# A two-layer attention block on one core: sums of the second softmax in float32r, and a new order at both ends of the run

## The chip, the cores and the metric

The kernel runs on one core of a Trainium2 chip. The metric is the device time in microseconds (us) of one launch of the whole program; lower is better. Ten runs of the kernel before are given, and one further execution that the hardware profiler took.

## The reference, cut to what matters

Eight images of 32 x 32 positions (N = 1024) and 512 channels pass through two layers; everything is float32.

```python
x = x + L0(_gn(x))      # 16 heads of 32: qkv = x @ w_qkv, softmax(q k^T * 32**-0.5) v, @ w_proj + b_proj
x = x + L1(_gn(x))      # 4 heads of 128: Wq, Wk, Wv, softmax((q k^T + position logits) / sqrt(128)) v, @ Wo
```

`_gn` is a group normalisation over groups of 16 channels. The position logits of layer 1 come from two learned tables, one for rows and one for columns of the image. A softmax is computed without subtracting a maximum: exponentials, their sums over the keys, and a division at the end.

## The kernel before, in words

**Layout.** The kernel works with channels on the partitions and tokens along the free axis, in tiles of 128 x 512. Eight blocks of 128 x 4 x 1024 floats (the pool `block`) hold activations; what is not needed for a while is written to DRAM (`put_away`, L213) and read back (`fetch`, L221). PSUM has eight banks: four as one tile `ps` for the first attention's scores, one `acc` for its output and its sums, and three named `bank` for everything else (L81).

**Projections.** Each 512 x 512 weight matrix is applied by a Strassen-like scheme with seven products instead of eight (`seven`, L341). Its inputs are the quarter blocks of the activation and four sums of these, made by four VectorE instructions of 128 x 1024 in `forms` (L324), and the matching four sums of the weights, made by `Matrix.add_up` (L137). A matrix takes 14 *products* (two units of seven); each is 8 matmuls of 32 columns, one per column group of the array (`by_columns`, L308).

**First attention** (`attention_0`, L519): 64 steps per batch (four groups of four heads, two halves of the queries, eight key tiles). A step issues 8 score matmuls into `ps` (L532), one exponential of 128 x 2048 on ScalarE (L540), 4 output matmuls into `acc` (L551) and one addition of 128 x 2048 to the running sums `es` on VectorE (L562). After eight steps `finish` (L568) multiplies `es` with a matrix of ones (L572), which both sums over the partitions and spreads the result, and `normalise` (L489) divides.

**Second attention** (`attention_1`, L637): also 64 steps per batch (four heads, two halves, eight key tiles). A step issues one score matmul of 128 x 512 in float32 (L647), one in float32r that adds the position logits (L648), an exponential of 128 x 512 (L650), one output matmul (L659) for the step before, and an addition to `es` (L670). After eight steps `finish` (L676) issues one float32 matmul of `ones` and `es` into a third of the `bank` tiles (L679), a copy to SBUF, two transposes with a reciprocal between, and a multiplication on GpSimd (L517).

**The order of the work** is written out by hand with Python generators. The main loop (L936) runs nine rounds. In round b, `side_by_side` (L862) steps through the first attention of batch b, and between its steps advances a chain of other work until `done` has caught up with `total`: the output projection of layer 0 for batch b-1 (`after_0`), that of layer 1 for batch b-2 (`after_1`), the second layer's projections for batch b-1 (`second`), its second attention, and the first layer's projections for batch b+1 (`before_0`). Each piece of that chain yields a cost: 2 for a product, and 0 for a step of the second attention. So the second attention of rounds 1 to 6 stands as one unbroken run of 64 steps between two steps of the first attention. In round 7, the last one with a first attention, `total` is 28 + 28 + 76 - 4 = 128, all first-attention steps stand beside the projections, and the second attention of batch 6 follows them. Round 8 has no first attention at all.

Inside the second attention of rounds 1 to 6, `woven(..., 4, 6)` (L850, L963) advances `load` (L696) of the next batch after every sixth step: transposes of the input, its statistics, the group normalisation, and then `forms` as a whole.

**The start** (`load_first`, L719) is different: the first batch is transposed on TensorE in two halves; the first half's four banks are copied by ScalarE (L745), the second half's by ScalarE and VectorE in turn (L747). Then come the statistics (L248), `put_away` to DRAM, the group normalisation in place, and `forms`. After that the program text fetches WQ and WK of layer 0 and lets VectorE make their sums (L146, called from L920). The framework's scheduler orders the instructions of each engine by when it thinks that they are ready, unless a helper (`issue_after`, `keep_in_program_order`) binds one to another.[...]

Of the kernel before, what the change touches and what calls it, by code (L numbers as in the profile page):

```python
# [17 lines left out]
P = 128  # L18
# [9 lines left out]
def quick_path(  # L28
# [52 lines left out]
    def bank(name, shape=None):  # L81
        return psum.tile(shape or [P, NB], F32, tag="bank", name=name, bufs=3)
# [1 line left out]

    ident = consts.tile([P, P], F32, tag="ident", name="ident")
    make_identity(nc, ident)
    ones = consts.tile([P, P], F32, tag="ones", name="ones")
    nc.gpsimd.memset(ones, 1.0)
    bproj_sb = consts.tile([P, CC], F32, tag="bproj_sb", name="bproj_sb")
    with nc.allow_non_contiguous_dma(reason="512 values, once"):  # L90
        nc.gpsimd.dma_start(bproj_sb, b_proj.rearrange("(cc p) -> p cc", p=P))
# [212 lines left out]
    in_place = [False]  # L304

    half_done = [None]

    def by_columns(out, weights, moving, start, stop, open_sum=False):  # L308

# [11 lines left out]
                tc.keep_in_program_order(ins)  # L321
        in_place[0] = False

    def forms(x, name):  # L324


        a11, a12 = x[:, :HC, :NB], x[:, HC:, :NB]
        a21, a22 = x[:, :HC, NB:], x[:, HC:, NB:]
        s1, s2, s4 = [
            mem.tile([P, HC, NB], F32, tag=f"form{i}", name=f"f{i}_{name}", bufs=1) for i in (1, 2, 4)  # L330
        ]
        nc.vector.tensor_add(s1, a21, a22)
        nc.vector.tensor_sub(s2, s1, a11)
        nc.vector.tensor_sub(a21, a11, a21)
        nc.vector.tensor_sub(s4, a12, s2)
        return [a11, a12, s4, a22, s1, s2, a21]

    def snapshot(tag, name):
        return mem.tile([P, NB], F32, tag=tag, name=name, bufs=3 if tag == "e1" else 2)
# [294 lines left out]
                if i % 2:  # L634
                    yield 0

    def attention_1(q, k, v, posT, b):  # L637

        steps = [(h, c, j) for h in range(H1) for c in range(NH) for j in range(NT)]
        state = {}  # L640

        def front(h, c, j):
            name = f"1_{b}_{h}_{c}_{j}"
            ps = bank(f"ps_{name}")
            keys = slice(j * P, (j + 1) * P)
            queries = slice(c * NB, (c + 1) * NB)
            nc.tensor.matmul(ps, k[h][:, keys], q[:, h, queries], start=True, stop=False)  # L647
            nc.tensor.matmul(ps, sel_flat[:, keys], posT[:, h, queries], start=False, stop=True)  # L648
            e = mem.tile([P, NB], F32, tag="e1", name=f"e_{name}", bufs=3)
            nc.scalar.activation(e, ps, AF.Exp, scale=1.0 / math.sqrt(D1))  # L650
            return e

        def back(h, c, j, e):
            name = f"1_{b}_{h}_{c}_{j}"
            if j == 0:
                state["acc"] = bank(f"acc_{name}")
                state["first"] = e
            acc = state["acc"]
            nc.tensor.matmul(  # L659
                acc,  # L660
                v[:, j, h * D1 : (h + 1) * D1],
                e,
                start=(j == 0),
                stop=(j == NT - 1),
            )
            if j == 1:
                state["esum"] = mem.tile([P, NB], F32, tag="es1", name=f"es_{name}", bufs=2)
                nc.vector.tensor_add(state["esum"], state["first"], e)  # L668
            elif j > 1:
                nc.vector.tensor_add(state["esum"], state["esum"], e)  # L670
            if j < NT - 1:
                return
            nc.scalar.copy(q[:, h, c * NB : (c + 1) * NB], acc)
            state["ended"] = (h, c, state["esum"])

        def finish(h, c, esum):  # L676
            name = f"1_{b}_{h}_{c}"
            su = bank(f"sums_{name}")
            nc.tensor.matmul(su, ones, esum, start=True, stop=True)  # L679
            normalise(q[:, h, c * NB : (c + 1) * NB], su, name)  # L680

        pending = None
        for at in steps:
            e = front(*at)
            ended = state.pop("ended", None)
            if pending is not None:
                back(*pending)
            pending = (*at, e)
            if ended is not None:
                finish(*ended)  # L690
            yield 0
        back(*pending)
        yield 0
        finish(*state.pop("ended"))

    def load(b, st):  # L696

        x = xT = None
        parts = [(cc, h) for cc in range(CC) for h in range(NH)]
        ahead = [load_blocks(b, *parts[i]) for i in range(2)]  # L700
        for i, (cc, h) in enumerate(parts):
            xs = ahead.pop(0)
            if i + 2 < len(parts):
# [12 lines left out]
        st["xn"] = forms(x, f"xn0_{b}")  # L716
        yield 0

    def load_first(st):  # L719

        rows = block("x_rows", [P, NT, C])
        for t in range(NT):
            queue = nc.scalar if t % 2 else nc.sync
            queue.dma_start(rows[:, t, :], xf[0, t * P : (t + 1) * P, :])
        WV0.fetch(nc.sync)
        x = block("x0T_0")
        xT = chunks(x)
        for h in range(NH):
            if h == 0:
                whole = psum.tile([P, CC, NB], F32, tag="ps", name="turned_0", bufs=1)  # L730
                banks = [whole[:, cc, :] for cc in range(CC)]
            else:
                banks = [bank(f"turned_1_{cc}") for cc in range(CC - 1)]
                banks.append(psum.tile([P, NB], F32, tag="acc", name="turned_1", bufs=1))
            for t in range(NT // NH):
                for cc in range(CC):
                    nc.tensor.transpose(
                        banks[cc][:, t * P : (t + 1) * P],
                        rows[:, h * (NT // NH) + t, cc * P : (cc + 1) * P],
                        ident,  # L740
                    )
            for cc in range(CC):
                part = xT[cc][:, h * NB : (h + 1) * NB]
                if h == 0 or cc % 2:
                    nc.scalar.copy(part, banks[cc])  # L745
                else:
                    nc.vector.tensor_copy(part, banks[cc])  # L747

        idle = psum.tile([P, CC, NB], F32, tag="ps", name="idle", bufs=1)
        for t in range(6):  # L750
            nc.tensor.matmul(idle[:, t % CC, :], ident, rows[:, t, :], start=True, stop=True)
        for cc in (1, 0, 3, 2):
            statistics(st, xT, cc, "0_0")
        st["kept"] = put_away(xT, "0_0")
        run(group_norm(st, xT, "0_0"))
        st["xn"] = forms(x, "xn0_0")
# [129 lines left out]
    def later(part, *args):  # L886

        yield from part(*args)
# [28 lines left out]
    WV0.add_up(nc.gpsimd, nc.gpsimd, keep=True)  # L917
    for m in (WQ0, WK0):
        m.fetch(nc.sync)
        m.add_up(nc.vector, nc.gpsimd, keep=True)  # L920
    fill_sel()
    stream = Stream(plan)

# [6 lines left out]
    def at_once(do):  # L930
        do()
        return
        yield

    run(before_first(states[0]))
    for b in range(B + 1):  # L936
# [11 lines left out]
        if last is not None:  # L948
            norm = norm_1(b - 1, last, (lambda: half_done[0]) if past is not None else None)
            rest.append(after_0(b - 1, last, forms_past if past is not None else None))  # L950
            total += PRODUCT
            if past is not None:
                rest.append(woven(later(after_1, b - 2, past), norm, 3, 3))
                total += PRODUCT
            else:
                rest.append(chain([ALONE], (cost + ALONE for cost in norm), marked()))
                total += 4 * ALONE
            rest.append(later(second, b - 1, last))
            total += SECOND
            if here is not None and coming is None:  # L960
                rest.append(at_once(forms_0))
                total -= 4
            rest.append(woven(later(lambda st: attention_1(*st.pop("at")), last), incoming, 4, 6))  # L963
        else:
            rest.append(woven(rest_of_first(here), incoming, 0, 2))
            total += PRODUCT
# [502 lines left out]
```

## Time and profile before

| what | value |
|---|---|
| median of 10 runs | 3904.27 us (3901.32 to 3908.26) |
| profiled execution | 3907.13 us, its span 3905.3 us |
| TensorE (PE) busy | 3811.1 us, 98% |
| VectorE (DVE) busy | 2518.1 us, 64% |
| ScalarE (ACT) busy | 1724.3 us, 44% |
| GpSimd (POOL) busy | 621.3 us, 16% |
| mean granted TensorE clock | 0.993 |

A float32 matmul shows as two matmul records, a float32r one as one. [...]what a matmul costs in a row of others is the distance from its start to the start of the next. A group's line gives the engine, the operation, output and inputs by name, the count, busy time and mean length, and then the idle time before it with what ended that.

### The profile page before, as it was taken

How to read it: one execution, taken by the hardware profiler on the slowest of the kernel's cores; microseconds unless marked ns; L12 is line 12 of the kernel's file. 1: busy time of each engine (PE TensorE's matmuls, PEld its weight loads, DVE VectorE, ACT ScalarE, POOL GpSimd, SP SyncE). 2: the span in 40 equal slices, each digit the busy share in tenths (PEclk: the TensorE clock that was granted, in tenths of full speed). 3: DMA queues.
4: the chain of work that ended last, by engine and by line, in shares of the span. 5: the costliest groups of instructions: out<-in, count | busy, mean ns of one | idle time of the engine just before them, and what ended most of it. 6: DMA issues, size and time to landing. Idle time of an engine off the chain costs nothing.

```text
span 3905.3 us, 79833 instructions
## 1 busy us (share of the span) xinstructions
PE 3811.1 (98%) x34478; PEld 1370.9 (35%) x34478; DVE 2518.1 (64%) x2905; ACT 1724.3 (44%) x1767; POOL 621.3 (16%) x400
## 2 busy tenths in 40 slices
PE   8999899999999999999999999999999999999998
PEld 3222244232442224432343323433234332244353
DVE  5767775577746867458664686656865568754544
ACT  2554453444434454344544445344453445543132
POOL 1341001121111210112101121111210112011101
PEclk9999999999999999999999999999999999999999
DMA  5231120133201422023220241103311123110401
GB/s 169 76 107 42 47 61 6 39 116 70 61 2 51 118 60 55 9 90 84 49 55 16 92 94 38 46 22 98 87 44 34 29 93 69 32 63 18 123 17 23
DMA packets 482984, 234.73 MB, mean 60 GB/s; under 512 B 269600, under 2 KB 461376, under 8 KB 481600
## 3 DMA queue, kind: packets, MB, share of 16 engines
q1 hardware_dynamic: 470992, 213.74, 20.3%
q0 software_dynamic: 2608, 13.70, 1.0%
q8 instruction: 274, 4.49, 0.5%
q10 hardware_dynamic: 9024, 2.10, 0.3%
q14 instruction: 86, 0.70, 0.1%
HBM read 170.72 MB, written 58.72 MB: 59 GB/s over the span
## 4 chain that ended last, share of the span: by engine, by line
PE 84%; DVE 9%; ACT 3%; issue 2%; POOL 1%; DMA 0%; SPq 0%; DVEq 0%; POOLq 0%; ACTq 0%
PE ps L647 11%; PE acc L659 11%; PE ps L532 11%; PE acc L551 10%; PE y_k L312 4%; PE y_v L312 4%; PE y_q L312 4%; PE ps L648 3%; PE x_v L312 3%; PE x_k L312 3%; PE z_k L312 3%; PE x_q L312 3%; PE z_v L312 3%; PE z_q L312 2%; ACT e L540 2%; DVE es L562 2%
## 5 line engine op out<-in xcount | busy, mean ns | idle before, releaser
L540 ACT ACTIVATE e<-ps 128x2048 f32<-128x2048 f32 x512 | 961.6, 1878 | 845.0 <-PE ps L532 608.1
L562 DVE TENSOR_TENSOR es<-es,e 128x2048 f32<-128x2048 f32 x384 | 890.7, 2319 | 400.3 <-ACT e L540 397.5
L532 PE MATMUL ps<-q,k 32*64 32x512 f32 x8192 | 578.1, 616 | 35.5 <-ACT e L540 35.4
L650 ACT ACTIVATE e<-ps 128x512 f32<-128x512 f32 x512 | 305.7, 597 | 586.2 <-PE ps L648 549.4
L551 PE MATMUL acc<-e,v 128*32 128x512 f32 x4096 | 548.0, 607 | 0.4 <-ACT su L495 0.4
L647 PE MATMUL ps<-q,k 128*128 128x512 f32 x1024 | 523.6, 593 | 0.3 <-DVE posT L633 0.3
L659 PE MATMUL acc<-e,v 128*128 128x512 f32 x1024 | 521.9, 592 | 0.0
L517 POOL TENSOR_TENSOR q<-q,su 128x512 f32<-128x512 f32 x128 | 214.3, 1674 | 1567.2 <-DVE su L513 1540.5
L670 DVE TENSOR_TENSOR es<-es,e 128x512 f32<-128x512 f32 x384 | 291.9, 760 | 264.0 <-ACT e L650 262.5
L648 PE MATMUL ps<-posT,sel 128*128 128x512 f32 x512 | 406.6, 794 | 0.0
L647 PEld LDWEIGHTS ps<-q,k 128*128 128x128 f32 x1024 | 193.6, 190 | 246.1 <-issue 240.6
L532 PEld LDWEIGHTS ps<-q,k 32*64 32x64 f32 x8192 | 120.5, 130 | 432.4 <-ACT e L540 215.3
L659 PEld LDWEIGHTS acc<-e,v 128*128 128x128 f32 x1024 | 193.1, 189 | 146.7 <-issue 105.0
L551 PEld LDWEIGHTS acc<-e,v 128*32 128x32 f32 x4096 | 81.5, 108 | 414.1 <-issue 366.3
L560 DVE TENSOR_TENSOR es<-e,e 128x2048 f32<-128x2048 f32 x64 | 174.4, 2725 | 40.3 <-ACT e L540 40.3
L497 DVE STREAM_TRANSPOSE tu<-su 128x512 f32<-128x512 f32 x128 | 90.6, 708 | 137.5 <-ACT su L495 137.3
L495 ACT COPY su<-sums 128x512 f32<-128x512 f32 x128 | 74.9, 585 | 152.5 <-PE sums L572 79.7
L648 PEld LDWEIGHTS ps<-posT,sel 128*128 128x128 f32 x512 | 97.3, 190 | 122.5 <-issue 122.5
L668 DVE TENSOR_TENSOR es<-e,e 128x512 f32<-128x512 f32 x64 | 44.2, 691 | 145.7 <-ACT e L650 145.7
L633 DVE TENSOR_TENSOR posT<-pp,posT 32x512 fp32r<-32x512 f32 x128 | 112.0, 875 | 32.1 <-ACT posT L628 30.8
L421 POOL TENSOR_TENSOR k<-b_k,p_k 128x512 f32<-128x512 f32 x32 | 51.2, 1599 | 476.9 <-ACT p_k L386 474.9
L628 ACT CAST posT<-pp 32x512 fp32r<-32x512 f32 x128 | 106.0, 828 | 45.3 <-PE pp L615 44.2
(195 smaller groups left out, 4517.9 us busy)
## 6 DMA issues: line engine op xcount, KB each, us to landing
w_qkv<-ws_qkv SPq DMA_DIRECT2D x168, 128.0 KB, 2.5
d<-x0T SPq DMA_DIRECT2D x32, 512.0 KB, 3.5
x1T<-d SPq DMA_DIRECT2D x32, 512.0 KB, 5.5
d<-x1T SPq DMA_DIRECT2D x32, 512.0 KB, 3.6
x2T<-d SPq DMA_DIRECT2D x32, 512.0 KB, 6.0
w_qkv<-in_L_conv_w_qkv SPq DMA_DIRECT2D x126, 128.0 KB, 2.2
out<-ot SPq DMA_DIRECT2D x240, 64.0 KB, 2.0
xs<-in_x SPq DMA_DIRECT2D x224, 64.0 KB, 2.6
```

Source lines behind the costliest of these rows:

```text
L312: ins = nc.tensor.matmul(out[columns, :], weights[:, columns], moving, start=start, stop=stop, skip_group_check=open_sum,)
L517: nc.gpsimd.tensor_tensor(dst, dst, su, op=ALU.mult)
L532: nc.tensor.matmul(ps[some, r, :], k[m][rows, j * P + 64 * i : j * P + 64 * i + 64], q[m][rows, h * NB : (h + 1) * NB], start=True, stop=True,
L540: nc.scalar.activation(e, ps, AF.Exp, scale=D0 ** -0.5)
L551: nc.tensor.matmul(acc[r * D0 : (r + 1) * D0, :], v[:, j, c0 : c0 + D0], e[:, r, :], start=(j == 0), stop=(j == NT - 1),)
L560: nc.vector.tensor_add(state["esum"], state["first"], e)
L562: nc.vector.tensor_add(state["esum"], state["esum"], e)
L647: nc.tensor.matmul(ps, k[h][:, keys], q[:, h, queries], start=True, stop=False)
L648: nc.tensor.matmul(ps, sel_flat[:, keys], posT[:, h, queries], start=False, stop=True)
L650: nc.scalar.activation(e, ps, AF.Exp, scale=1.0 / math.sqrt(D1))
L659: nc.tensor.matmul(acc, v[:, j, h * D1 : (h + 1) * D1], e, start=(j == 0), stop=(j == NT - 1),)
L670: nc.vector.tensor_add(state["esum"], state["esum"], e)
```

## The change

It has four parts.

- **Last first-layer attention.** In round 7 the first 32 steps of the second attention now cost 1 each instead of 0, and `total` becomes 28 + 28 + 76 + 32 = 164. So `side_by_side` places about a fifth of the first attention's steps among these 32. `forms_0`, which needs the finished first attention, moves to after step 40 of the second attention.
- **The second layer's sums.** `finish` copies `es` to float32r on ScalarE (`greater`), subtracts that from `es` on VectorE (`rest`), and two steps later issues two float32r matmuls with `ones`, into the four-bank `ps` tile, which the first attention isn't using at that time. The first three finishes of round 7 keep the old form, since there it is in use.
- **The next batch's forms.** `forms` becomes a generator, `forming`, that yields after each of its four instructions, each bound behind the latest addition to `es`. `load` is advanced every fifth step instead of every sixth.
- **The start.** ScalarE copies all eight banks, in the order 0, 2, 1, 3; statistics follow the same order; the sums of WQ and WK are bound behind the last instruction of `forms`.

```diff
+    ones_r = consts.tile([P, P], F32R, tag="ones", name="ones")
+    nc.gpsimd.memset(ones_r.bitcast(F32), 1.0)
+    ones = ones_r.bitcast(F32)
...
-    def forms(x, name):
+    def forming(x, name, behind=None):
...
+        for op, out, one, other in (
+            (nc.vector.tensor_add, s1, a21, a22),
+            (nc.vector.tensor_sub, s2, s1, a11),
+            (nc.vector.tensor_sub, a21, a11, a21),
+            (nc.vector.tensor_sub, s4, a12, s2),
+        ):
+
+            late = behind() if behind is not None else None
+            with tc.issue_after(late.ins) if late is not None else nullcontext():
+                last_form[0] = op(out, one, other)
+            yield 0
         return [a11, a12, s4, a22, s1, s2, a21]
...
-    def attention_1(q, k, v, posT, b):
+    def attention_1(q, k, v, posT, b, beside=0):
...
         def finish(h, c, esum):
             name = f"1_{b}_{h}_{c}"
-            su = bank(f"sums_{name}")
-            nc.tensor.matmul(su, ones, esum, start=True, stop=True)
+            if (h * NH + c + 1) * NT < beside:
+                su = bank(f"sums_{name}")
+                nc.tensor.matmul(su, ones, esum, start=True, stop=True)
+                normalise(q[:, h, c * NB : (c + 1) * NB], su, name)
+                return
+
+            yield
+
+            greater = mem.tile([P, NB], F32R, tag="rec", name=f"sg_{name}", bufs=2)
+            nc.scalar.copy(greater, esum)
+            rest = mem.tile([P, NB], F32R, tag="rec", name=f"sr_{name}", bufs=2)
+            nc.vector.tensor_sub(rest, esum, greater.bitcast(F32))
+
+            yield
+            yield
+
+            su = psum.tile([P, HB, NB], F32, tag="ps", name=f"sums_{name}", bufs=1)[:, 0, :]
+            nc.tensor.matmul(su, ones_r, greater, start=True, stop=False)
+            nc.tensor.matmul(su, ones_r, rest, start=False, stop=True)
             normalise(q[:, h, c * NB : (c + 1) * NB], su, name)

         pending = None
+        ending = []
         for at in steps:
             e = front(*at)
-            ended = state.pop("ended", None)
             if pending is not None:
                 back(*pending)
             pending = (*at, e)
-            if ended is not None:
-                finish(*ended)
+            for part in ending:
+                next(part, None)
+            if "ended" in state:
+                ending = [finish(*state.pop("ended"))]
+                next(ending[0], None)
             yield 0
         back(*pending)
         yield 0
-        finish(*state.pop("ended"))
+        run(finish(*state.pop("ended")))
...
-        st["xn"] = forms(x, f"xn0_{b}")
-        yield 0
+        st["xn"] = yield from forming(x, f"xn0_{b}", lambda: added[0])
...
-            for cc in range(CC):
+            for cc in (0, 2, 1, 3):
                 part = xT[cc][:, h * NB : (h + 1) * NB]
-                if h == 0 or cc % 2:
-                    nc.scalar.copy(part, banks[cc])
-                else:
-                    nc.vector.tensor_copy(part, banks[cc])
+                nc.scalar.copy(part, banks[cc])
...
-        for cc in (1, 0, 3, 2):
+        for cc in (0, 2, 1, 3):
             statistics(st, xT, cc, "0_0")
...
-        m.add_up(nc.vector, nc.gpsimd, keep=True)
+
+        with tc.issue_after(last_form[0].ins):
+            m.add_up(nc.vector, nc.gpsimd, keep=True)
...
-            if here is not None and coming is None:
-                rest.append(at_once(forms_0))
-                total -= 4
-            rest.append(woven(later(lambda st: attention_1(*st.pop("at")), last), incoming, 4, 6))
+            shared = here is not None and coming is None
+            attention = later(
+                lambda st, steps: attention_1(*st.pop("at"), steps), last, H1 * NT if shared else 0
+            )
+            if shared:
+
+                attention = woven(
+                    (int(at < H1 * NT) for at, _ in enumerate(attention)),
+                    at_once(forms_0),
+                    H1 * NT + NT,
+                    H1 * NH * NT,
+                )
+                total += H1 * NT
+            rest.append(woven(attention, incoming, 4, 5))
```

More of the change, by code (lines that the diff above doesn't have):

```diff
@@ L86, in quick_path @@
     make_identity(nc, ident)
-    ones = consts.tile([P, P], F32, tag="ones", name="ones")
-    nc.gpsimd.memset(ones, 1.0)
+    ones_r = consts.tile([P, P], F32R, tag="ones", name="ones")
+    nc.gpsimd.memset(ones_r.bitcast(F32), 1.0)
+    ones = ones_r.bitcast(F32)
     bproj_sb = consts.tile([P, CC], F32, tag="bproj_sb", name="bproj_sb")
@@ L306, in quick_path @@
     half_done = [None]
+    last_form = [None]
+    added = [None]
     def by_columns(out, weights, moving, start, stop, open_sum=False):
@@ L331, in forms, with whole @@
         ]
[L332 to L335, printed above, removed]
-        return [a11, a12, s4, a22, s1, s2, a21]
+        for op, out, one, other in (
[8 more added lines that the diff above has]
+            yield 0
+        return [a11, a12, s4, a22, s1, s2, a21]
+    def forms(x, name):
+        got = []
+        def whole():
+            got.append((yield from forming(x, name)))
+        run(whole())
+        return got[0]
     def snapshot(tag, name):
@@ L669, in back @@
             elif j > 1:
-                nc.vector.tensor_add(state["esum"], state["esum"], e)
+                added[0] = nc.vector.tensor_add(state["esum"], state["esum"], e)
             if j < NT - 1:
```

## The prediction

> **What bounds the kernel now.** I read the page's busy times and its chain of waits, then busy time by stretch, then the order of matmuls inside the second attention, and last VectorE's timeline at the start.
>
> ```profile
> span 3905.3 us, 79833 instructions
> ...
> PE 3811.1 (98%) x34478; PEld 1370.9 (35%) x34478; DVE 2518.1 (64%) x2905; ACT 1724.3 (44%) x1767; POOL 621.3 (16%) x400
> ...
> PE 84%; DVE 9%; ACT 3%; issue 2%; POOL 1%; DMA 0%; SPq 0%; DVEq 0%; POOLq 0%; ACTq 0%
> ```
>
> TensorE is the bound: 98% busy, 84% of the chain. An edit gains only by removing matmul time or by filling the 94 us in which TensorE idles. Where these lie, TensorE alone, in stretches (stretch, length, busy time, granted clock):
>
> ```profile
> 1033.60:1165.40 131.80, 131.80 (x344) 1.00 0.11 27
> 2704.50:2926.10 221.60, 218.90 (x2521) 1.00 0.27 66
> 3176.50:3463.00 286.50, 271.98 (x3076) 0.99 0.21 56
> 3463.00:3594.90 131.90, 131.90 (x343) 1.00 0.05 19
> ```
>
> The first and fourth are runs of the second attention: no idle time at all. The second is round 6 beside projections: 2.7 us idle. The third is round 7: 14.5 us idle, of which the waits for its stretch give 9.6 to the wide exponential (L540) and 2.6 to the last sums. That is all the first part can win.
>
> Inside the second attention (start, length, engine, line, ...):
>
> ```profile
> 1083.24 1.02 PE L647 MATMUL ps<-q,k 128*128 128x512 f32 x2
> 1083.70 0.79 PE L648 MATMUL ps<-posT,sel 128*128 128x512 f32 x1
> 1084.33 1.02 PE L659 MATMUL acc<-e,v 128*128 128x512 f32 x2
> 1085.19 1.02 PE L679 MATMUL sums<-es,ones 128*128 128x512 f32 x2
> 1086.05 1.02 PE L647 MATMUL ps<-q,k 128*128 128x512 f32 x2
> ```
>
> Starts, not lengths, give the cost. Sums: 1086.05 - 1085.19 = 0.86 us. A whole step is 1.945 us (1081.29 to 1083.24), two float32 matmuls take 1.71 of it, so the float32r one takes 0.23.
>
> The start, on VectorE:
>
> ```profile
> 14.67 0.20 DVE L249 BATCH_NORM_AGGREGATE mv<-st 128x2 f32<-128x12 f32 x1
> 16.88 1.68 DVE L146 TENSOR_TENSOR prep_qkv<-prep_qkv 128x512 f32<-128x512 f32 x1 [2.02 <-DMA prep_qkv<-in_L_conv_w_qkv]
> ...
> 24.55 0.16 DVE L285 SCALAR_TENSOR_TENSOR var<-back 128x4 f32<-128x4 f32 x1
> 25.88 2.98 DVE L292 TENSOR_SCALAR x0T<-x0T,back,rstd 128x1024 f32<-128x1024 f32 x4 [1.16 <-POOL rstd L289]
> 28.77 0.69 DVE L146 TENSOR_TENSOR prep_qkv<-prep_qkv 128x512 f32<-128x512 f32 x1
> 29.38 1.22 DVE L332 TENSOR_TENSOR f_xn<-x0T 128x1024 f32<-128x1024 f32 x1
> ```
>
> The statistics stand behind a sum of weights that waits for its DMA; TensorE stands idle for 10.39 us before its first product at 26.79.
>
> [...]0.23 for one float32r pass, 0.43 for each half of a float32 matmul. [...]sums followed by 32-column products take 0.95 us (1164.42 to 1165.37), not 0.86. [...]on SP's queue WQ lands at 16.86 and the four stores of x0T, issued after it, 1.1 to 1.3 us apart from 18.13 to 21.82. [...]
>
> **Part 1, round 7.** The built order has 53 first-attention steps before the second attention's first step and 11 among its next 31. The same 70 products (5 matrices of 14) now share 53 steps instead of 64. No matmul is removed, so the gain is idle time only. Two points are measured: 64 steps with 70 products idle 14.5 us, of which 2.6 is the wait of the last sums at the end of the stretch; round 6 has 42 steps with its 70 products and idles 2.7. In a line between 11.9 and 2.7, 53 steps give 7.3. The end wait goes, since second-attention matmuls now stand there. Among the mixed steps TensorE needs 2.03 + 2.8 x 1.95 = 7.5 us per first-attention step, VectorE 2.3 + 2.8 x 0.76 = 4.4, ScalarE 1.9 + 2.8 x 0.6 = 3.6, so I expect little idleness there, 0.5. But in the built order a single one of the eight score matmuls stands twice in front of full-width sums; alone, it takes its whole 0.86 us: 1.7. New idle time 7.3 + 0.5 + 1.7 = 9.5; gain 14.5 - 9.5 = **5.0**. Bounds: -2 (mixed steps stall as the old ones did) to 12. The moved `forms_0`, 4.9 us of VectorE, lands where VectorE is under half busy (59 of 132) and TensorE waits for nothing; without that cover it would cost up to 4.9. On SP's queue the fetch of x1T (four DMAs, landing in 6 us) moves behind weights that are released as TensorE goes on; the data is wanted tens of us later: nothing.
>
> **Part 2, the sums.** 61 of 64 are changed. Two float32r passes: [...]0.47 by the trace's 0.23; a weight load of 0.19 (L648's) hides under each. I take 0.47; saved 0.86 - 0.47 = 0.39 in the 53 finishes that have more steps behind them: 20.7. The added copy (an ACT copy of that size takes 0.585; a cast, L628, 0.83) and subtraction (0.69; a float32r one, L633, 0.875) wait behind exponentials and additions; queued behind the copy is the next exponential, behind the subtraction the next addition. By the old run's times, around 575 us, `rest` is ready at 578.2 and its matmul would stand at 580.7: 2.5 us of cover, so nothing. Without it each 1 us of lateness costs 53.
>
> At the **end of a run** there is no cover. The built order is: last `acc`, *one* 32-column product matmul, both sums, the other seven. The last addition ends at 1164.12, copy 1164.73, `rest` 1165.5. The lone matmul takes 0.86, its column group running by itself, then comes a wait of about 0.1, sums 0.47, and two more changes of tiling at 0.1. Against 0.86 before, that is 0.86 + 0.1 + 0.47 + 0.2 - 0.86 = 0.77 lost, 7 times: -5.4. In round 8 the end is followed by a chain through ScalarE, VectorE and GpSimd for which TensorE idles anyway; it starts 0.75 later: -0.75. Sum 20.7 - 5.4 - 0.75 = **14.5**. Bounds: 2 (passes of 0.28, casts at the dear rates, 1.5 lost at each end) to 25 ([...]ends that gain too).
>
> **Part 3, the next batch's forms.** 4 instructions of 1.22 us spread over VectorE inside a run without idle time, before and after: **0**. They end about five steps (10 us) before the run does; if that were lost, the first product would wait up to 1.2 us, 6 times. The bound upward is 0 too: there is no wait to remove.
>
> **Part 4, the start.** VectorE loses two copies and gets statistics without the weights' sums: it would finish `var` near 16.5 instead of 24.7. GpSimd's `rstd` stands behind WV's sums and the issue of their store there (until 18.9), so about 20 instead of 25.8. But the normalisation overwrites x0T, and so waits for its stores. WK's fetch of 1 MB now stands ahead of them in SP's queue: at WQ's pace (2.5 us) that moves them from 18.1...21.8 to 20.7...24.5, and the store of WV's sums (landing 26.35 before) takes a share: I take 27 for the last. Then the second of the forms, which TensorE's third product needs, is ready at 27 + 0.75 + 2.4 = 30.2 instead of 32.3. Before, TensorE's 14 products end at 55.58, at 1.73 each as if begun at 31.4; now two are done by 30.2, as if begun at 26.7: 4.7. Against that, the eight sums of WQ and WK (0.65 each) now stand on VectorE ahead of the first evacuation of y, until 38, and the product that accumulates onto y would be due at 36.9: 1.6 lost. **3**; bounds 0 to 7.
>
> **Sum.** 5.0 + 14.5 + 0 + 3 = 22.5. Against the profiled execution (3907.1, 1.8 more than its span) 3884.6; the profiled one is 2.9 over the median of the ten, so from 3904.3: **3882**.
>
> **Rivals.**
> - *Nothing is lost at the edges.* TensorE overlaps the lone matmul with what follows, stores land early, mixed steps have no idle time: 10 + 22 + 7 = 39, 3865. For it: VectorE has slack everywhere. Against: waits in the built order[...].
> - *The edits hardly reach their place.* Round 7 keeps its idle time (VectorE's work is the same, 222 of 286 us), stores hold the start: 0 + 10.5 + 0.5 = 11, 3893. For it: VectorE's load beside 53 steps is nearly what it was beside 64.
> - *`rest` comes late every time, slower.* The sums stand in TensorE's order; if copy and subtraction slip behind the next batch's normalisation and forms, each finish stalls TensorE. From 22.5 / 53 = 0.42 us per finish, that is `rest` 2.9 us later than laid out, the kernel is slower; at 4 us later, 53 x 1.5 = 80 is lost: 3962. Against: VectorE is 57% busy there (75 of 132), and no single instruction exceeds 1.3 us.
>
> **Chances.** Forecast 0.56, first rival 0.20, second 0.20, third 0.04. A measurement of this kernel can tell about 0.2% (7.8 us) from no change. The forecast's own spread is 3875 to 3889; half the first rival's cases and most of the second's are taken in to reach 8 in 10: 3864 to 3895. Faster 0.92: the first three cases, less the slowest of the second; same 0.05; slower 0.03.
>
> **What would show it.** Right: runs of the second attention of about 129.5 us instead of 131.8, sums starting 0.47 before what follows, one gap near 0.1 and a lone x_q matmul at each end; idle time of 9 to 10 us in round 7; the first product near 21 to 23 and WQ's first at about 52.5. Wrong: idle time before the sums inside a run, or float32r passes over 0.3 apart; and the sum would be wrong if round 7 with its 32 steps isn't 5 us shorter than before.

## The result, and the profile after

The changed kernel takes **3875.25 us** (median of 8 runs, 3871.06 to 3880.73), the kernel before 3903.7 us over the 28 runs that stand beside it. The ratio is 0.9931, with a 95% interval from 0.9922 to 0.994: 28 us or 0.7% less. The forecast was 3882 with a range of 3864 to 3895, so the sign and the range held. The gain is 6 us larger than the 22.5 that was worked out, and its parts don't lie where the sum put them.

The profiled execution took 3880.94 us. On its page, the span and the busy times:

```profile
span 3879.1 us, 79880 instructions
...
PE 3797.7 (98%) x34478; PEld 1373.7 (35%) x34478; DVE 2556.8 (66%) x2964; ACT 1761.1 (45%) x1830; POOL 614.2 (16%) x400
```

TensorE remains the bound, with exactly as many matmul records as before: a float32 matmul leaves two, and so do the two float32r ones that replace it. What was removed is time in the records and idle time between them. In stretches (stretch, length, busy time of TensorE, granted clock, DMA share, GB/s):

```profile
1026.88:1155.14 128.26, 128.26 (x339) 1.00 0.11 27
2690.10:2909.60 219.50, 216.79 (x2504) 1.00 0.27 66
3161.40:3405.00 243.60, 240.57 (x2777) 1.00 0.23 58
3405.00:3564.40 159.40, 159.40 (x622) 1.00 0.07 26
```

The first is a run of the second attention from its first scores to the end of its last output matmul, again without idle time; before, such a run took 130.97 (1033.61 to 1164.58). The second is round 6, with 2.7 us of idle time as before. The third and fourth together are round 7: 3.0 us of idle time in the part beside projections, where 14.5 had been and 9.5 were forecast, and none in the part that the two attentions share.

A round is measured here from the start of its first product to that of the next round's. The changed kernel is 3.3 us ahead at WQ's first product and 3.4 at the start of round 1. Round 1 gains 3.3, of which 1.4 isn't the edit's: TensorE runs 10.2 us of that round at half clock, and 17.1 in the trace before. Rounds 2 to 6 gain 1.9 each (16.2 at the end of round 6), round 7 gains 14.2 (30.4), and round 8 gives 4.1 back: 26.3, the difference of the two spans. Of the 14.2, 0.95 is only moved: the last sums of round 7's run stood ahead of round 8's first product before, and stand behind its first matmul now.

Inside the second attention, the new sums (start, length, engine, line, operation):

```profile
1080.72 1.02 PE L679 MATMUL acc<-e,v 128*128 128x512 f32 x2
1081.17 0.80 PE L715 MATMUL sums<-sg,ones 128*128 128x512 f32 x1
1081.81 0.40 PE L716 MATMUL sums<-sr,ones 128*128 128x512 f32 x1
1082.05 1.02 PE L667 MATMUL ps<-q,k 128*128 128x512 f32 x2
```

From the output matmul's start to the next score matmul's are 1082.05 - 1080.72 = 1.33 us; without sums between them it is 0.86 (1084.33 to 1085.19 in the prediction's lines of the kernel before). The pair costs 0.47, as forecast, in place of 0.86. No wait stands before it.

At the end of a run, before and after:

```profile
1162.61 1.97 PE L659 MATMUL acc<-e,v 128*128 128x512 f32 x4
1164.42 1.02 PE L679 MATMUL sums<-es,ones 128*128 128x512 f32 x2
1165.37 1.92 PE L312 MATMUL x_q<-x0T,w_qkv 128*32 128x512 f32 x16
1167.22 0.69 PE L532 MATMUL ps<-q,k 32*64 32x512 f32 x8
```

```profile
1153.16 1.97 PE L679 MATMUL acc<-e,v 128*128 128x512 f32 x4
1155.07 1.05 PE L316 MATMUL x_q<-x0T,w_qkv 128*32 128x512 f32 x2
1156.04 0.51 PE L715 MATMUL sums<-sg,ones 128*128 128x512 f32 x1
1156.39 0.39 PE L716 MATMUL sums<-sr,ones 128*128 128x512 f32 x1
1156.71 1.92 PE L316 MATMUL x_q<-x0T,w_qkv 128*32 128x512 f32 x14
1158.55 0.69 PE L552 MATMUL ps<-q,k 32*64 32x512 f32 x8
```

The lone x_q matmul (two records) holds TensorE for 0.97 us, the sums for 0.67, the other seven for 1.84 together. From the start of the last outputs to the next scores are 5.39 us; before, 1162.61 to 1167.22, 4.61. So 0.78 is lost at each end; 0.77 was forecast. The gap of about 0.1 that the forecast had there doesn't show; the lone matmul is longer by as much than the 0.86 it was given. The 0.67 is what the forecast's 0.47 and its two times 0.1 for a change of tiling come to; the 0.1 was its estimate from one place in the trace before, 0.95 us for sums ahead of 32-column products against 0.86 for those inside a run.

The start, on VectorE:

```profile
19.11 0.16 DVE L286 SCALAR_TENSOR_TENSOR var<-back 128x4 f32<-128x4 f32 x1
20.83 0.81 DVE L293 TENSOR_SCALAR x0T<-x0T,back,rstd 128x1024 f32<-128x1024 f32 x1 [1.56 <-DMA d<-x0T]
...
27.19 0.81 DVE L293 TENSOR_SCALAR x0T<-x0T,back,rstd 128x1024 f32<-128x1024 f32 x1 [2.87 <-DMA d<-x0T]
28.04 1.23 DVE L345 TENSOR_TENSOR f_xn<-x0T 128x1024 f32<-128x1024 f32 x1
29.30 1.23 DVE L345 TENSOR_TENSOR f_xn<-f_xn,x0T 128x1024 f32<-128x1024 f32 x1
```

The normalisation now waits for the stores of what it overwrites (the bracket names the DMA d<-x0T), the last until 27.19, and the second form is ready at 30.5: 27 and 30.2 were forecast.

### The profile page after: what moved, and what is told of

Same layout as the page of the kernel before. It is cut to its first block, busy times and chain, and to the rows that moved or that the text cites. A ratio compares the mean times of both kernels' runs of the same rounds, so it can differ in the third digit from the quotient of the medians.

```text
span 3879.1 us, 79880 instructions
## 1 busy us (share of the span) xinstructions
PE 3797.7 (98%) x34478; PEld 1373.7 (35%) x34478; DVE 2556.8 (66%) x2964; ACT 1761.1 (45%) x1830; POOL 614.2 (16%) x400
## 5 line engine op out<-in xcount | busy, mean ns | idle before, releaser
L441 POOL TENSOR_TENSOR v<-b_v,p_v 128x512 f32<-128x512 f32 x32 | 50.8, 1586 | 443.1 <-ACT p_v L406 440.4
```

## The experiments

They start from the kernel before with one part of the change alone, then with two, then from the changed kernel with one detail altered. Each text on record states its own theories. In a sum of medians each difference carries some 4 us either way, so the traces' own distances are read beside the times.

**Part 1 alone.** Only the round-7 sharing and the place of `forms_0` are taken from the diff (its last hunk).

> The kernel before with part 1 alone (32 second-attention steps of cost 1, the first attention's last steps among them, the old sums). Theory A, from the trace after: the idle time of round 7 falls from 14.5 us to about 3 because 53 instead of 64 steps share the projections, and nothing else of the change is needed for it: 9 to 12 us less than before. Theory B, as the prediction had it: 5 us less, and what the trace after shows beyond that in round 7 comes of the other parts together (the freed third bank in the mixed steps). If B, this run gains 4 to 6.

Measured: 3890.77 us against 3900.63, ratio 0.9972 (0.9962 to 0.9982), 9.9 us less. Theory A. In round 7, from its first to the next round's first product, the trace is 14.1 us shorter. What TensorE waited for beside the projections (engine, tile and line, releaser: us, times, longest), the longest of the kernel before and then all but one of this run:

```profile
PE ps L532 <- ACT e L540: 9.6, 8, 2.7
PE sums L572 <- DVE es L562: 2.6, 1, 2.6
```

```profile
PE ps L532 <- ACT e L540: 1.4, 2, 1.2
PE sums L572 <- DVE es L562: 1.3, 1, 1.3
```

Of 9.6 us for the wide exponential and 2.6 for the last sums, 1.4 and 1.3 are left, with another 0.3 elsewhere. Part 1 by itself takes away the idle time, 11.5 us of it where 5.0 was forecast. The trace gains 2.6 more than that: 1.7 because the trace before has a stretch of half clock in round 7 and this one has none, and 0.9 that isn't traced.

**Part 2 alone.** `ones_r`, the new `finish` and its stepping, and nothing else; without part 1 all 64 finishes are of the new form.

> The kernel before with part 2 alone (the float32r sums, in every round). Theory A, the prediction's working: 56 finishes with steps behind them at 0.39 us, seven run ends at -0.77, the last at -0.75, so 15.7 us less than before; a run of the second attention of 128.3 us up to its last acc. Theory B: the sums also free a tile of the bank pool, and waits outside the runs shrink; then 18 or more. Theory C: the float32r pair costs more once the other parts are away (rest late because the forms stand as a block on VectorE): 10 or less.

Measured: 3897.87 us, ratio 0.9993 (0.9984 to 1.0001): 2.8 us, hardly to be told from nothing. Theory A is out. Theory C has the size right, and not the place: nothing waits for the sums. Runs of the second attention up to the last output take 129.7 us in rounds 1 to 6, against 128.26 in rounds 7 and 8, where no next batch's `load` stands beside them. VectorE, ScalarE and TensorE around the one idle place of the run in round 2:

```profile
1073.36 2.30 DVE L335 TENSOR_TENSOR x0T<-x0T 128x1024 f32<-128x1024 f32 x1
...
1075.58 0.68 DVE L671 TENSOR_TENSOR es<-es,e 128x512 f32<-128x512 f32 x1
...
1076.18 1.21 DVE L336 TENSOR_TENSOR f_xn<-x0T,f_xn 128x1024 f32<-128x1024 f32 x1
...
1077.31 0.68 DVE L671 TENSOR_TENSOR es<-es,e 128x512 f32<-128x512 f32 x1
1078.08 0.62 ACT L688 CAST sg<-es 128x512 fp32r<-128x512 f32 x1 [3.31 <-DVE es L671]
1078.61 0.59 ACT L651 ACTIVATE e<-ps 128x512 f32<-128x512 f32 x1
...
1079.25 1.12 PE L660 MATMUL acc<-e,v 128*128 128x512 f32 x2 [1.22 <-ACT e L651]
```

It is read from below. TensorE waits 1.22 us for an exponential. The exponential stands on ScalarE behind the copy `sg`, and the copy, after 3.31 us of idling, waits for the last addition to `es`. That addition stands on VectorE behind the fourth form, another addition and the third form. The third form is also slow: it takes 2.30 us where a form by itself takes 1.2, and so it is in all six runs (2.29 to 2.30). A multiplication on GpSimd started 0.36 us ahead of it each time (the last section has what this does). So about 1.1 us of the lateness comes of that meeting and the rest of the order; no run takes the two apart. In the kernel before, the forms make the additions late too (one starts at 1078.33, though its exponential ended at 1077.34), but there every exponential of that stretch waits for its scores alone, and TensorE doesn't idle.

**Part 3 alone.** `forming` and the fifth step instead of the sixth.

> The kernel before with part 3 alone (the next batch's forms one by one, load advanced every fifth step). Theory A: the run of the second attention has no idle time before, so nothing: within 1.5 us of before. Theory B: the forms as a block delayed the first steps after the run, and spreading them takes 1 us from each of six rounds: 5 us less.

Measured: 3901.18 us, ratio 0.9997 (0.9989 to 1.0006): nothing, as forecast. Theory A.

**Parts 2 and 3 together.**

> The kernel before with parts 2 and 3 together (float32r sums, and the next batch's forms spread over VectorE), parts 1 and 4 left out. Alone, part 2 gave 2.8 us and part 3 nothing. Theory A: they are worth more together than apart, because the forms as a block on VectorE delay the last addition, ScalarE's copy waits for it, and the next exponential, queued behind the copy, makes the output matmul late by 1.2 us once in each of six runs. Then the runs of the second attention in rounds 1 to 6 shrink from 129.7 to 128.3 us, and the time is 11 to 13 us below the kernel before. Theory B: parts 2 and 3 don't act on each other; runs stay at 129.7 and the time is 2 to 4 us below the kernel before. Theory C: the prediction's 14.5 for part 2 was right, and part 3 adds something besides: 14.5 or more.

Measured: 3891.64 us against 3901.23, ratio 0.9974 (0.9964 to 0.9984): 9.6 us less, where the two alone sum to about 2.3. The runs of all rounds are 128.2 to 128.3 us long and have no idle time. Theory A holds in the trace, and in time but for its last 1.4 us; B is out. Every form inside the runs takes 1.2 us here, so the run takes away the block and the meeting with GpSimd at once; nor does it tell the spreading from the fifth step.

**Part 2 with the copy moved.** If the wait goes by way of the exponential behind the copy, it should go without part 3 too, once the copy stands behind that exponential:

```diff
-            nc.scalar.activation(e, ps, AF.Exp, ...)
+            risen.append(nc.scalar.activation(e, ps, AF.Exp, ...))
...
-            nc.scalar.copy(greater, esum)
+            with tc.issue_after(risen[-2].ins):
+                nc.scalar.copy(greater, esum)
```

> The kernel before with part 2 alone, but with ScalarE's copy bound behind the first exponential of the next group, so that no exponential which TensorE needs next stands behind the copy. The forms remain a block. Theory A (the stall goes from the late addition by way of the copy to the exponential behind it): the wait of 1.22 us for the exponential in each of six runs is gone, runs of 128.3 instead of 129.7 us, 11 to 13 us below the kernel before. Theory B (the stall comes from VectorE's lateness itself, through the exponentials' buffers or through rest): the wait stays near 1.2 us or moves before the sums, and the time stays 2 to 4 us below the kernel before.

Measured: 3893.01 us, ratio 0.9978 (0.9968 to 0.9988): 8.2 us less. The forms are a block as before, and the wait for the exponential is gone:

```profile
1074.75 0.62 ACT L690 CAST sg<-es 128x512 fp32r<-128x512 f32 x1 [1.31 <-DVE es L672]
1075.27 0.58 ACT L675 COPY q<-acc 128x512 f32<-128x512 f32 x1
...
1075.90 1.13 PE L649 MATMUL ps<-q,k 128*128 128x512 f32 x2 [0.29 <-ACT q L675]
```

But now the copy of `acc` to `q` is what stands behind the cast, and the next scores wait 0.29 us for the bank that it empties. Runs are 128.8 us (128.4 in round 1), between 129.7 and 128.3: of the 1.46 us lost in each run, 0.9 came back, while the third form still takes 2.3. So the mechanism is A's, with a second, smaller victim behind the same copy that A hadn't named.

**Part 4 alone.** The order of the start's copies and statistics, and the binding of the weights' sums.

> The kernel before with part 4 alone (the start). Theory A: 3.3 us less at WQ's first product, 4.8 by the end of round 0, as the trace after has it. Theory B: the gain at the start is eaten by round 0, where TensorE waits for GpSimd and VectorE and not for its own past: less than 2 us less than before.

Measured: 3899.0 us, ratio 0.9994 (0.9986 to 1.0003), 1.6 us less. Theory B has the size, but that round 0 eats the gain isn't shown. Its trace has WQ's first product 3.4 us earlier than that of before, but in the traces of parts 1, 2 and 3 alone, which leave the start as it was, that product also comes 0.9 to 1.1 earlier, and 2.3 in that of parts 2 and 3. So 1 to 2.5 us by the traces, and 1.6 by the time, which can't tell either from nothing. Theory A's 4.8 isn't reached at the end of round 0 in the trace after, where it is 3.4, but in round 1, by the clock.

By the ratios, part 1 (0.28%), parts 2 and 3 (0.26%) and part 4 (0.06%) sum to 0.60%, against 0.69% for the whole change: within the intervals, and no run has other pairs of parts together.

**How many steps are shared in round 7.** In the changed kernel, the number 32 in `attention`'s steps, `total` and the place of `forms_0` is replaced by 0, 16 or 48:

```diff
-                lambda st, steps: attention_1(*st.pop("at"), steps), last, H1 * NT if shared else 0
+                lambda st, steps: attention_1(*st.pop("at"), steps), last, 16 if shared else 0
```

> The changed kernel, but no first-attention step among the second attention's in round 7: all 64 stand among the projections; the move of the forms of layer 0 is kept. Theory A (idle time falls in a line with the number of first-attention steps among the 70 products, as the prediction has it): about 12 us of idle time in round 7 against 3.0, so some 9 us slower than the changed kernel, 19 us below the kernel before. Theory B (a threshold somewhere between 53 and 64 steps): the same here, to be told apart by a number of steps in between. Theory C (it was the move of the forms, 4.9 us of VectorE, that freed round 7): idle time at most 5 us, within 3 us of the changed kernel.

> The changed kernel with 16 of the second attention's steps shared in round 7 in place of 32: 58 first-attention steps stand beside the 70 products, between the 64 of the run without sharing (11.4 us of idle time in its trace) and the 53 of the changed kernel (3.0). Theory A (idle time is a line in the number of steps, as the prediction drew it): 6.8 us idle, some 4 us slower than the changed kernel. Theory B (idle time is a few single waits, each where an addition of the first attention stands on VectorE behind a long piece of other work; the number of steps only shifts which meet): no line; the single wait of 6.3 us is there or is not, idle time at most 4.5 or at least 9.

> The changed kernel with 48 shared steps: 48 first-attention steps beside the products, 16 among the second attention's. Theory A (a line): idle time goes on falling to about 0, some 3 us faster than the changed kernel. Theory B (single waits): the two waits of 1.2 and 1.3 us that the changed kernel still has don't depend on the number; idle time stays at 2 to 4 us, and each first-attention step among the second attention's may add a lone score matmul; within 3 us of the changed kernel.

Measured, each against its own runs of before:

| shared steps | first-attention steps beside the 70 products | idle in round 7, us | ratio to before |
|---|---|---|---|
| 0 | 64 | 11.4 | 0.9945 (0.9932 to 0.9959) |
| 16 | 58 | 9.5 | 0.9953 (0.994 to 0.9967) |
| 32 (as changed) | 53 | 3.0 | 0.9931 (0.9922 to 0.994) |
| 48 | 48 | 3.3 | 0.994 (0.9926 to 0.9953) |

That is no line: from 64 to 58 steps 1.9 us less, from 58 to 53 6.5 less, then nothing more. Nor was it only the move of `forms_0`, which share 0 has too. B's picture, single waits that come and go with the count, is right: with 16 the one of 6.33 us is gone, and waits of 3.1, 1.9 and 1.5 make up most of its 9.5. (B's text had 9 or more for the case in which the 6.33 stays, so its number held for another reason than its own.) The longest, in the kernel with no shared steps, on VectorE, ScalarE and TensorE:

```profile
3235.41 2.98 DVE L293 TENSOR_SCALAR x1T<-x1T,back,rstd 128x1024 f32<-128x1024 f32 x4 [1.20 <-POOL rstd L290]
3238.30 2.28 DVE L580 TENSOR_TENSOR es<-e,e 128x2048 f32<-128x2048 f32 x1
...
3240.68 1.88 ACT L560 ACTIVATE e<-ps 128x2048 f32<-128x2048 f32 x1 [7.45 <-DVE es L580]
...
3242.61 1.16 PE L552 MATMUL ps<-q,k 32*64 32x512 f32 x8 [6.33 <-ACT e L560]
```

An addition of the first attention stands behind a whole normalisation, which itself waited 1.2 us for GpSimd; the exponential waits 7.45 us for the buffer that the addition frees, and the scores wait for the exponential. In times, the intervals of 16 and 32 just touch and all others overlap, and 16 and 48 read slower than 32 by more than their idle time says, 16 perhaps because its trace has a stretch of half clock in round 7 (1.7 us). Which number is best isn't settled.

**The end of a run.** The changed kernel with the last finish of each run in the old form:

```diff
-            if (h * NH + c + 1) * NT < beside:
+            if (h * NH + c + 1) * NT < beside or (h, c) == (H1 - 1, NH - 1):
```

> The changed kernel, but the last finish of each run of the second attention in the old form, one float32 matmul directly behind the last output matmul, so that the product's eight matmuls aren't split. Theory A (the split costs what the prediction says, 0.77 us an end; the trace has 0.78 more from the last output matmul to the next scores than before): six ends and round 7's give 5 to 6 us, 33 to 35 below the kernel before, and the lone x_q matmul is gone. Theory B (the lone matmul stands in time that the old form spends waiting for the last addition): no more than 2 us below the changed kernel, with a wait before the sums.

Measured: 3868.58 us against 3901.23, ratio 0.9917 (0.9903 to 0.993). The end of the run in round 2:

```profile
1150.82 1.97 PE L679 MATMUL acc<-e,v 128*128 128x512 f32 x4
1152.63 1.02 PE L700 MATMUL sums<-es,ones 128*128 128x512 f32 x2
1153.58 1.92 PE L316 MATMUL x_q<-x0T,w_qkv 128*32 128x512 f32 x16
1155.44 1.11 PE L552 MATMUL ps<-q,k 32*64 32x512 f32 x16
```

From the last outputs to the next scores it is 4.62 us again, and each of the rounds 2 to 6 gains 2.7 us over before instead of 1.9. Theory A.

A step further, the sums are kept in float32r but held back until the following product is whole: `finish` is left hanging after its subtraction in a list `owed`, and `product` runs it after its last matmul. These sums go to a tile of `bank`; rounds 7 and 8 end in the old form.

```diff
             stream.ahead(i)
+            if owed:
+                run(owed.pop())
...
-        run(finish(*state.pop("ended")))
+        last = finish(*state.pop("ended"))
+        if b > B - 3:
+            run(last)
+        else:
+            next(last)
+            next(last)
+            owed.append(last)
```

> The changed kernel, but in rounds 1 to 6 the last sums of the run, as two float32r matmuls into a bank of their own, stand behind the whole first product of eight matmuls that follows, so that no product is split; rounds 7 and 8 end in the old form. Theory A (an end loses by the split alone): against the run with all ends in the old form, 0.39 us less at each of six ends, so runs with their ends 2.3 us shorter in all, some 35 us below the kernel before. Theory B (the wait for rest or for a free bank takes the place of the split): a wait before the sums or before y, no gain over the old ends, 32 below the kernel before or less.

Measured: 3869.11 us against 3902.75, ratio 0.9916 (0.9902 to 0.9929), the same as the old ends. The end of the run in round 2:

```profile
1149.30 1.92 PE L318 MATMUL x_q<-x0T,w_qkv 128*32 128x512 f32 x16
1151.15 0.50 PE L723 MATMUL sums<-sg,ones 128*128 128x512 f32 x1
1151.49 0.40 PE L724 MATMUL sums<-sr,ones 128*128 128x512 f32 x1
1151.82 1.11 PE L556 MATMUL ps<-q,k 32*64 32x512 f32 x16
```

There is no wait, but the pair takes 1151.82 - 1151.15 = 0.67 us here, between matmuls of other tilings, as at the ends of the changed kernel, and not 0.47. The end takes 4.43 us (from 1147.39) against 4.62: 0.2 saved and not 0.39, 1.1 us over six ends, below what times can show. Neither theory had that. Both kernels lie 5 to 6 us below the changed one by the ratios to before; the intervals overlap, but the 0.8 us per round by the traces, some 5 for six rounds, say the same.

## Why the prediction was right or wrong

**The sum.** It is nearer than its terms. By the traces the start gave 3.4 us (3 forecast), rounds 1 to 6 without the clock 11.4 (11.8), round 7 without the moved sums 13.2 (6.6), and round 8 with them -3.2 (+1.2). Rounds 7 and 8 are each off by more than 4 us in opposite directions, and that they offset each other is luck.

**Part 1, the step that was too small.** Forecast 5.0, measured 9.9 in time (7 to 15 by the interval) and 11.5 in idle time. The term that failed is "in a line between 11.9 and 2.7, 53 steps give 7.3": there is no line. Idle time is a handful of places where an addition to `es` meets a long piece on VectorE, and at 53 steps the schedule has only two of over 1 us left. A second term was put at nothing, the clock: "that is all the first part can win" counts idle time alone. The eight traces with 9.5 us or more of idle time in round 7 all have TensorE at half clock there for 3.4 us or longer (3.4 before, 6.8 with no shared steps), and the five with some 3 us never. So the bound of 12 holds for the 9.9 and the 11.5, and not for the 14.1 between the traces of before and of part 1 alone. The two lone score matmuls that the prediction read off the order are there (0.99 and 1.00 us each before full-width sums, instead of 0.13 inside a group of eight), so the 1.7 for them was right, though they show as busy and not as idle time, as the forecast's sum counted them. Idle time 11.5, clock 1.7, four sums 1.6 and the moved sums 0.95, less 1.7 for the lone matmuls, make 14.0 of the 14.2 that round 7 gained.

**Part 2, right in size, on a condition that part 3 supplied.** The pair at 0.47, the 0.39 per finish and the 0.77 per end were measured at 0.47, 0.39 and 0.78, and each of rounds 1 to 6 should gain 7 x 0.39 - 0.78 = 1.95; rounds 2 to 6 show 1.9. What failed is the sentence on cover: "2.5 us of cover, so nothing". It measured how late `rest` may be for the sums. The wait that came with part 2 was a different one, of the exponential queued behind the copy, which the prediction named as queued there and then didn't price. Nor is it so that "no single instruction exceeds 1.3 us" on VectorE there: in the trace before, an addition to `es` takes 1.75 in the midst of that run (at 1075.52). Part 2 alone therefore gave 2.8 of its 14.5.

**Part 3, wrong.** "The bound upward is 0 too: there is no wait to remove" was true of the kernel before, where it gives nothing. In the changed kernel there is a wait to remove: part 2 makes one of 1.46 us in each of six runs, and part 3 takes it away, 8.8 us by the traces and 9.6 - 2.8 = 6.8 by the times. The forecast's sum didn't suffer, because part 2 had been priced as if the wait didn't exist; the two errors cancel, which is luck too.

**Part 4.** 3 forecast, 1 to 2.5 found, with the stores at the stated times. TensorE waits 1.1 us for the second form; the wait for an evacuation of y, put at 1.6, is 0.35.

**What wasn't in the sum.** Round 8 gives 4.1 us back, where 7 x 0.39 - 0.75 = 2.0 more was forecast. The starts of the same instructions show where. At its first product 1.0 goes, which is round 7's last sums, moved there. Around the second y_wo product 1.7 goes: the wait for `a_wo` before it is 1.63 us instead of 0.57, because of a meeting of VectorE with GpSimd (next section), and 0.6 stays open. At WQ of layer 1 the wait is 0.2 longer, and 1.7 is lost behind it: the clock stayed full before, after 2.90 us of idling, and is at half for 3.4 us now, after 3.09. The run itself gives 2.7. Behind it 1.3 goes, where 0.75 was forecast, and 0.9 in a stretch of half clock that lasts 6.8 us instead of 3.4. The clock also differs between executions of one kernel: of the kernel before, those beside the run with old ends have a mean granted clock from 0.993, over a span of 3904.7 us, to 0.995, over spans of 3897.3 to 3899.4.

**The rivals.** "Nothing is lost at the edges" had round 7 nearly right and the ends wrong. "The edits hardly reach their place" is out for round 7, whose idle time fell to 3.0 us, and right about the stores at the start. "`rest` comes late every time" had the right place, ScalarE and VectorE beside the next batch's work; with part 2 alone something did come late there, the last addition and not `rest`, and once in a run, not at each finish.

## What to carry to other kernels

An operation that you add to an engine's queue can be late because its own input is late, and make what is queued behind it late too: part 2's copy waited 3.31 us for an addition, and TensorE then 1.22 for the exponential behind the copy. Look for the lateness of what it *reads*, not only for when its result is wanted. Price parts of a change together where one brings a new reader of something that another moves: two parts worth 2.8 and 0 alone were worth 9.6. And idle time that consists of a few meetings of two queues needn't fall in a line with the load (here 11.4, 9.5, 3.0 and 3.3 us for 64, 58, 53 and 48 steps): list the waits one by one, with what stands ahead of the releaser, before interpolating.

## What the runs showed of the hardware

**An idle TensorE paid twice in some places and not in others.** Two waits in the kernel before, TensorE alone, each in two neighbouring windows of 3.41 us. The first wait is 2.65 us long (until 3291.27), the second 2.90 (until 3660.72):

```profile
3287.76:3291.17 3.41, 0.86 (x8) 1.00 0.13 38
3291.17:3294.58 3.41, 3.31 (x24) 0.50 0.02 5
3656.40:3659.81 3.41, 1.42 (x16) 1.00 0.75 115
3659.81:3663.22 3.41, 2.50 (x24) 1.00 0.80 236
```

The shorter wait was followed by half clock for 3.4 us, 1.7 us lost on top of the 2.65; the longer was not. In each of the 13 traces all changes of the clock lie whole multiples of 3.413 us apart, and the windows here begin and end at such places. From 10 us after the start to the last matmul, every window at full clock in which TensorE was busy for less than 0.40 of the time was followed by half clock (0.86 of 3.41 is 0.25), none with more than 0.50 was, and in between both occur (1.42 of 3.41 is 0.42). At half clock, windows with less than 0.77 were followed by another such, and those with more than 0.80 by full clock. Of the twelve waits of 2.1 to 3.1 us in the traces of before and after, seven were followed by 3.4 us at half clock, 1.7 us lost, and five by none. Each of the seven has a window that was busy for 0.38 or less; at the five, no window was below 0.42. Traces of different kernels differ by such steps in round 0 too, where none of the edits but the start's can reach: 20.5 us at half clock in the trace before, 13.7 in that of part 1 alone. So the medians, not single traces, have to decide.

**VectorE and GpSimd held each other up.** The third addition to x1T and GpSimd's addition to x2T in round 8, before and then after:

```profile
3621.53 0.74 DVE L438 SCALAR_TENSOR_TENSOR x1T<-p_wp,bproj_sb,x1T 128x512 f32<-128x512 f32 x1
3621.55 1.85 POOL L431 TENSOR_TENSOR x2T<-x2T,p_wo 128x512 f32<-128x512 f32 x1 [4.62 <-issue]
```

```profile
3592.74 1.29 POOL L451 TENSOR_TENSOR x2T<-x2T,p_wo 128x512 f32<-128x512 f32 x1 [4.56 <-ACT p_wo L387]
3592.78 1.80 DVE L458 SCALAR_TENSOR_TENSOR x1T<-p_wp,bproj_sb,x1T 128x512 f32<-128x512 f32 x1
```

In both, the one that started first took its usual time, and the other took longer: 1.85 instead of 1.29 on GpSimd, 1.80 instead of 0.74 on VectorE. A shift by some 0.05 us turned the order round, and the 1.06 us are those by which `a_wo`, and with it TensorE's second y_wo product, came later. All 13 traces fall into these two cases: six with part 1 and 16 or more shared steps have the second, the other seven the first. The forms show the same. In all 13 traces, the 313 forms of 128 x 1024 that start while GpSimd is at an element-wise operation take 1.65 to 2.31 us, and the other 1351 take 1.15 to 1.23.

**A float32r matmul pair cost 0.47 us among full-width matmuls and 0.67 between 32-column ones** (in the trace after, 1.33 - 0.86 from 1080.72 on, and 1156.04 to 1156.71), and one 32-column matmul alone in front of full-width ones cost 0.97 (from 1155.07), against 1.84 for seven in a row (from 1156.71).
